# A pairwise bilinear kernel: when the first store of a group leaves, and its last three fields sent in nine row slices

## The chip, the cores and the metric

The kernel runs on one core of one Trainium2 chip. The metric is the device time of one execution in microseconds. Three runs of the kernel before gave 1286.73, 1286.80 and 1287.43 us; the median is 1286.8 us. One further execution was profiled; it took 1287.24 us.

## What is computed

The input `x` holds 4096 samples of 32 fields with 64 numbers each, in float32, and `W` is a 64 x 64 matrix. For each pair of fields i < j the output is the product, number by number, of field i with field j times W:

```
vid = jnp.einsum('bfd,de->bfe', x, W)
idx_i, idx_j = jnp.triu_indices(F_, k=1)
return x[:, idx_i, :] * vid[:, idx_j, :]
```

There are 32 * 31 / 2 = 496 pairs a sample, so the output is 15.5 times as large as the input: 520 MB are written and 33.6 MB are read.

## The kernel before

**Tiles.** The samples are cut into 16 tiles of 256. A tile lies in memory with 2 x 64 numbers of the embedding on the 128 partitions (two half-batches of 128 samples share a tile) and 128 samples along a row. One field of a tile is then a unit of 128 partitions x 512 bytes, 64 KB. The one buffer `mem` has 445 such units on the chip. It holds inputs (32 units a tile, at the places of `XPLACE`) and outputs (at the places of `SLOTS`) together, and parts of it are used again and again.

**Work of a tile.** Eight matmuls (line 172) multiply 32 fields by a matrix that has W twice on its diagonal, into `vid` in PSUM. Then VectorE (DVE in the profile) makes the 496 products (line 196), several pairs in one instruction, in an order given by `by_block`. It writes them into the output slots one after another. When a slot is full (`at == end`), one transfer from SyncE's queue (SP) takes it to the output (line 199). `SLOTS` lists 70 slots of 32 to 127 units with their places in `mem`; a third number in an entry is a seam, at which DVE's instructions are split. A slot's place is written again as soon as the stores that read it, as far as they overlap the new piece, have landed.

**Loads.** The tiles are loaded in three groups (`GROUPS`): tiles 0 to 5 at the start, tiles 6 to 10 when tile 4's products are issued, and tiles 15 to 11 later on. A group's load is cut in pieces (`CUTS`), each piece a transfer of its own (line 153). The pairs of numbers in `CUTS` are ranges of units of the group: the last load of the first group, 64 units, goes as 38 and 26; the second group's 160 units as 127, 7 and 26; the third's as 127, 7 and 26 from the top down.

**Order around the change.** The orders of SP's and DVE's instructions are as written in the program (`manual_schedule`). SP issues all transfers, loads and stores, in one queue. After a group's load, `pieces` holds its transfers, and the first store that follows gets an extra dependency by `behind(store, pieces[-2])`: it is issued only when the last piece but one has landed. At this point one piece, 26 units, is still on its way. `pieces` is then emptied, so no other store has such a wait. In what follows, the three places where a load is followed by such a store are called boundaries. The stores concerned are slot 0 (96 units), slot 22 (96 units) and slot 44 (120 units).

The framework gives every transfer a semaphore that tells of its landing. In the trace, 81 transfers (11 loads and 70 stores) use eight semaphores by turns. Each landing counts 16, one for each DMA engine.

Of the kernel before, what the change touches and what calls it, by code (L numbers as in the profile page):

```python
# [21 lines left out]
    [[6, 7, 8, 9, 10]],  # L22
    [[15, 14, 13, 12, 11]],
]
CUTS = [[None, [(0, 38), (38, 64)]], [(0, 127), (127, 134), (134, 160)], [(33, 160), (26, 33), (0, 26)]]
XPLACE = [317, 349, 381, 413, 32, 0, 285, 317, 349, 381, 413, 128, 96, 64, 32, 0]


# [9 lines left out]
    (126, 247), (127, 96), (109, 223), (112, 333), (127, 158), (127, 285), (127, 64, 94),  # L38
    (127, 192, 93), (124, 320), (120, 48), (127, 190), (124, 317), (125, 158),
]  # L40


PAD = 24
# [9 lines left out]
def by_block():  # L53


    def within(lo):
        yield "step", lo, 2, 1, 0
        for k in range(2):
            yield "step", lo, 4, 2, k
        for i in (lo, lo + 8):  # L60
            yield "row", i + 4, i, 4, 4
        yield "row", lo + 8, lo, 8, 8

    yield from within(0)
    yield "row", 16, 0, 16, 16
    yield from within(16)


def products(blocks, at=0):

    for kind, a, b, c, d in blocks:
        if kind == "row":
            rows, n, i0, di, j0, dj = c, d, b, 0, a, 1
        else:
            rows, n, i0, di, j0, dj = 16 // b, c, a, b, a + c + d, b
        r = k = 0
        while r < rows:
            room = BREAKS[bisect_right(BREAKS, at)] - at
            if k or room < n:
                m, w = 1, min(n - k, room)  # L80
            else:
                m, w = min(rows - r, room // n), n
            yield at, m, w, i0 + r * di + k, di, j0 + r * dj, dj
            at += m * w
            if k + w == n:
                r, k = r + m, 0
            else:
                k += w
# [10 lines left out]
@with_exitstack  # L99
def pairwise_bilinear_kernel(  # L100
    ctx: ExitStack,
    tc: tile.TileContext,
    x0: bass.AP,
    x: bass.AP,
    out: bass.AP,
):

    nc = tc.nc
    NT = sum(len(tiles) for group in GROUPS for tiles in group)
    F = x0.shape[1] - 1 - PAD0
    D = P // 2
    NP = F * (F - 1) // 2

    BANK = 512 // C


    ctx.enter_context(tc.manual_schedule(engines={mybir.EngineType.SP, mybir.EngineType.DVE}))

    const = ctx.enter_context(tc.tile_pool(name="const", bufs=1))
    psum = ctx.enter_context(
        tc.tile_pool(name="ps", bufs=1, space=bass.MemoryType.PSUM)
    )
    vid = psum.tile([P, F, C], F32)

    mem = const.tile([P, UNITS, C], F32)


    w2 = const.tile([P, P], F32)


    place = XPLACE[0]
    nc.sync.dma_start(
        out=mem.rearrange("p u c -> p (u c)")[:, place * C - D : (place + F // 2) * C],
        in_=x0.rearrange("p u c -> p (u c)")[:, C - D : (1 + F // 2) * C],
    )
    nc.sync.dma_start(out=mem[:, place + F // 2 : place + F, :], in_=x0[:, 1 + F // 2 : 1 + F, :])  # L140
    nc.vector.memset(w2, 0.0)  # L141
    for half in (slice(0, D), slice(D, P)):
        nc.vector.tensor_copy(w2[half, half], mem[half, place - 1, C - D :])  # L143
    loaded = 1

    def load(tiles, cuts=()):
        nonlocal loaded
        n = len(tiles) * F
        place = XPLACE[tiles[0]]
        at = (loaded - 1) * F  # L150
        loaded += len(tiles)
        return [
            nc.sync.dma_start(out=mem[:, place + lo : place + hi, :], in_=x[:, at + lo : at + hi, :])  # L153
            for lo, hi in cuts or [(0, n)]
        ]

    ready = mybir.DependencyInfo(mybir.DependencyClass.Sync, mybir.DependencyReason.DATA)

    def behind(later, earlier):
        tc.add_manual_dep(later.ins, earlier.ins.name, ready, reason="issued when that has landed")  # L160

    pieces = []
    groups, cuts = iter(GROUPS), iter(CUTS)
    for tiles, parts in zip(next(groups)[1:], next(cuts)):
        pieces = load(tiles, parts)

    for t in range(NT):
        xt = mem[:, XPLACE[t] : XPLACE[t] + F, :]


        for b in range(0, F, BANK):
            nc.tensor.matmul(  # L172
                vid[:, b : b + BANK, :],
                lhsT=w2,
                rhs=xt[:, b : b + BANK, :],
                start=True,
                stop=True,
            )

        for at, m, w, i, di, j, dj in products(by_block(), t * NP):  # L180
            slot = bisect_right(STARTS, at) - 1
            n = m * w
            begin, end = STARTS[slot], STARTS[slot + 1]
            ot = mem[:, SLOTS[slot][1] : SLOTS[slot][1] + SLOTS[slot][0], :]
            o = ot[:, at - begin : at - begin + n, :]
            if m == 1:
                left = xt[:, i : i + w, :]
                right = vid[:, j : j + 1, :].to_broadcast([P, w, C])
            else:
                o = o.rearrange("p (m w) c -> p m w c", m=m)  # L190
                right = vid[:, j : j + (m - 1) * dj + 1 : dj, :].unsqueeze(2).to_broadcast([P, m, w, C])
                if di == 0:
                    left = xt[:, i : i + w, :].unsqueeze(1).to_broadcast([P, m, w, C])
                else:
                    left = xt.rearrange("p (m d) c -> p m d c", d=di)[:, i // di : i // di + m, i % di : i % di + w, :]
            nc.vector.tensor_tensor(o, left, right, ALU.mult)  # L196
            at += n
            if at == end:
                store = nc.sync.dma_start(out=out[:, begin:end, :], in_=ot)  # L199
                if pieces:  # L200
                    behind(store, pieces[-2])
                    pieces.clear()


        if t + 2 == loaded < NT:
            (tiles,) = next(groups)
            pieces = load(tiles, next(cuts))
# [45 lines left out]
```

## Time and profile before

| | |
|---|---|
| median of three runs | 1286.8 us |
| the profiled execution, its own time | 1287.24 us |
| its span, first to last instruction | 1285.5 us |
| DVE busy | 1084.0 us (84%), 348 instructions |
| TensorE (PE) busy | 231.1 us (18%) |
| transfers' packets and bytes | 11,664 packets, 553.7 MB |
| chain that ended last | DVE 47%, DMA 44%, issue 6% |
| DVE's waits for stores | 164.2 us, 33 times, longest 21.8 us |

The times are microseconds from the start of the span. "Landing" is when a transfer's semaphore has reached its value; since 16 engines carry a transfer and each reports for itself, a transfer has 16 landings, and their spread is how far the engines have drifted apart. A packet is what one engine moves in one go, here one row of a transfer: a transfer of 128 rows gives each of the 16 engines eight packets. The trace has the start, duration and size of each packet, but not the number of its engine. A transfer's issue on SP (some 0.3 us) is not the transfer itself, which goes on long after.

The three boundaries in the trace, in us:

| | first store issued | load's last piece landed, first to last engine | first store landed, first to last engine |
|---|---|---|---|
| first | 28.78 | 31.99 to 33.91 | 46.45 to 48.42 |
| second | 426.51 | 429.45 to 432.34 | 443.98 to 446.92 |
| third | 829.50 | 831.80 to 834.84 | 849.93 to 852.96 |

### The profile page before, as it was taken

The numbers are of one execution on the slowest core, as the hardware profiler recorded it, in microseconds if no ns is written. First come the engines' busy times: TensorE is split into PE (matmuls) and PEld (weight loads), VectorE is DVE, ScalarE is ACT, GpSimd is POOL, SyncE is SP. The second block draws the span as 40 slices with busy tenths as digits, with TensorE's granted clock in tenths as the row PEclk, the third lists the DMA queues.
The fourth block names the chain that finished last, engine by engine and source line by source line (L and its number), as shares of the span: only waits on it lengthen the run. The fifth ranks groups of instructions, "written<-read, shape, count | busy, mean of one in ns | idle before, by whom it ended". The sixth has DMA issues, their size and how long they took to land.

```text
span 1285.5 us, 1143 instructions
## 1 busy us (share of the span) xinstructions
PE 231.1 (18%) x256; PEld 67.7 (5%) x256; DVE 1084.0 (84%) x348; POOL 0.2 (0%) x4
## 2 busy tenths in 40 slices
PE   5031121303120212040311211103122130312000
PEld 1000000100000000010000000000000010000000
DVE  6889998899967389899799992849998889999952
POOL 0000000000000000000000000000000000000000
PEclk8555565556555556555565555556555555555555
DMA  9999999999999999999999999999999999999998
GB/s 400 438 429 438 436 428 438 431 435 436 432 430 439 416 433 425 445 430 433 439 427 441 435 429 436 419 432 429 440 432 440 429 430 441 429 441 430 434 436 370
DMA packets 11670, 553.75 MB, mean 431 GB/s; under 512 B 1296, under 2 KB 1296, under 8 KB 1552
## 3 DMA queue, kind: packets, MB, share of 16 engines
q1 hardware_dynamic: 11664, 553.69, 99.8%
q8 instruction: 2, 0.03, 0.0%
q14 instruction: 4, 0.03, 0.0%
HBM read 33.59 MB, written 520.09 MB: 431 GB/s over the span
## 4 chain that ended last, share of the span: by engine, by line
DVE 47%; DMA 44%; issue 6%; PE 0%; DVEq 0%; SPq 0%
DVE mem L196 47%; DMA out_dram<-mem 41%; DMA mem<-in_r_x_dram 3%; PE vid L172 0%; DVEq L241 0%; DVEq L196 0%; DVE w L143 0%; SPq L153 0%; DVEq L143 0%; SPq L199 0%
## 5 line engine op out<-in xcount | busy, mean ns | idle before, releaser
L196 DVE TENSOR_TENSOR mem<-mem,vid 128x1024 f32<-128x1024 f32 (+17 forms) x345 | 1083.4, 3212 | 170.5 <-DMA out_dram<-mem 164.2
L172 PE MATMUL vid<-mem,w 128*128 128x512 f32 x256 | 231.1, 1039 | 951.3 <-DVE mem L196 843.8
L172 PEld LDWEIGHTS vid<-mem,w 128*128 128x128 f32 x256 | 67.7, 306 | 1113.5 <-DVE mem L196 1011.9
L143 DVE COPY w<-mem 64x64 f32<-64x64 f32 x2 | 0.4, 190 | 5.0 <-DMA mem<-in_r_x_dram 4.9
L141 DVE MEMSET w<- 128x128 f32 x1 | 0.2, 165 | 0.8 <-PEq L221 0.8
L221 POOL MEMSET const-bfloat16-1.0<- 128x1 bf16 x1 | 0.1, 101 | 0.0
L221 POOL MEMSET const-uint8-127<- 128x1 uint8 x1 | 0.1, 101 | 0.0
L221 POOL MEMSET const-float32-0.0<- 128x1 f32 x1 | 0.1, 98 | 0.2 <-issue 0.2
L221 POOL MEMSET const-float32-1.0<- 128x1 f32 x1 | 0.1, 98 | 0.0
## 6 DMA issues: line engine op xcount, KB each, us to landing
out_dram<-mem SPq DMA_DIRECT2D x15, 8128.0 KB, 27.4
out_dram<-mem SPq DMA_DIRECT2D x14, 7680.0 KB, 24.9
out_dram<-mem SPq DMA_DIRECT2D x6, 7168.0 KB, 26.2
out_dram<-mem SPq DMA_DIRECT2D x5, 7936.0 KB, 28.2
out_dram<-mem SPq DMA_DIRECT2D x3, 7424.0 KB, 22.6
out_dram<-mem SPq DMA_DIRECT2D x3, 5888.0 KB, 20.9
mem<-in_r_x_dram SPq DMA_DIRECT2D x2, 8128.0 KB, 37.6
out_dram<-mem SPq DMA_DIRECT2D x2, 8064.0 KB, 24.3
```

The source lines that it names most:

```text
L141: nc.vector.memset(w2, 0.0)
L143: nc.vector.tensor_copy(w2[half, half], mem[half, place - 1, C - D :])
L172: nc.tensor.matmul(vid[:, b : b + BANK, :], lhsT=w2, rhs=xt[:, b : b + BANK, :], start=True, stop=True,)
L196: nc.vector.tensor_tensor(o, left, right, ALU.mult)
L221: nc = _bacc.Bacc("TRN2", target_bir_lowering=False, num_devices=1, dynamic_dma_scratch_size=512)
```

## The change

It has two parts. The cuts of the loads move, so that the last piece, which is still on its way when the first store is issued, has 13 units at the first boundary and 20 at the others, in place of 26; the second piece of the later groups has 13 units in place of 7. And the first store of each group, the one with the extra dependency, is cut in two: all units but the last three go out in one transfer of 128 partitions, and the last three in nine transfers that take 64, 14, 12, 10, 8, 8, 6, 4 and 2 partitions (together 128). The nine follow in SP's program right behind the main transfer. The extra dependency is on the main transfer alone. All other stores stay as they are. The kernel then has 108 transfers in place of 81.

```diff
-CUTS = [[None, [(0, 38), (38, 64)]], [(0, 127), (127, 134), (134, 160)], [(33, 160), (26, 33), (0, 26)]]
+CUTS = [[None, [(0, 51), (51, 64)]], [(0, 127), (127, 140), (140, 160)], [(33, 160), (20, 33), (0, 20)]]
...
+TAIL = 3
+ROWS = [64, 14, 12, 10, 8, 8, 6, 4, 2]
...
             if at == end:
-                store = nc.sync.dma_start(out=out[:, begin:end, :], in_=ot)
+                cut = SLOTS[slot][0] - (TAIL if pieces else 0)
+                store = nc.sync.dma_start(out=out[:, begin : begin + cut, :], in_=ot[:, :cut, :])
+                if begin + cut < end:
+                    for lo, n in zip(accumulate([0, *ROWS]), ROWS):
+                        rows = slice(lo, lo + n)
+                        nc.sync.dma_start(out=out[rows, begin + cut : end, :], in_=ot[rows, cut:, :])
                 if pieces:
                     behind(store, pieces[-2])
                     pieces.clear()
```

## The prediction

> **What bounds the kernel now.** I read the queue table first, because the strip of 40 slices shows the DMA engines at 9 in all slices but the last.
>
> ```profile
> q1 hardware_dynamic: 11664, 553.69, 99.8%
> HBM read 33.59 MB, written 520.09 MB: 431 GB/s over the span
> ```
>
> One queue carries every load and store, and its packets fill 99.8% of 16 engines' span. A packet of 65,024 bytes takes 2.40 us by the packet records (27 GB/s an engine), so the bytes alone set the time. The packet times sum to 1282.4 us an engine; with each size at its usual (20th percentile) duration they would sum to 1278.3. So 4.1 us is all that can come from faster packets. Some more lies in skew: the 16 landings of one transfer spread, 0.8 us in the first loads and 2.88 us (1281.72 to 1284.60) in the last store. The slowest engine sets the end.
>
> Next the chain of waits, for the places where a load hands over to the first store of a group (three "boundaries").
>
> ```profile
> 12.52 16.27 DVE mem L196 x7
> 28.78 19.64 DMA out_dram<-mem
> 48.42 0.03 issue
> ```
>
> The store leaves at 28.78 and the last engine's part lands at 48.42. DVE's data was ready earlier: what held it was the load, as SP's own waits say.
>
> ```profile
> SPq L199 <- DVE mem L196: 1104.4, 67, 32.5
> SPq L199 <- DMA mem<-in_r_x_dram: 96.8, 3, 35.8
> ```
>
> Three waits for a load, one a boundary; all other stores wait for DVE. The issues around the boundaries:
>
> ```profile
> 28.78 0.35 SPq L199 DMA_DIRECT2D out_dram<-mem  x1
> ...
> 41.95 0.34 SPq L199 DMA_DIRECT2D out_dram<-mem  x1
> ```
> ```profile
> 426.51 0.82 SPq L199 DMA_DIRECT2D out_dram<-mem  x2
> ```
> ```profile
> 833.50 0.34 SPq L199 DMA_DIRECT2D out_dram<-mem  x1
> ```
>
> The second store of a group is issued at 41.95, 426.91 and 833.50: 6.5, 20.0 and 19.5 us before the first store's last landing (48.42, 446.92, 852.96). So today the engines pass from the first store to the second without a hole. Last, line 199 in the view by source line:
>
> ```profile
> L199 SPq DMA_DIRECT2D out_dram<-mem x70: 332/332/423, 28.8 to 1260.2; - x70
> L199 SPq EVENT_SEMAPHORE  x60: 17/17/28, 28.7 to 1229.7; - x60
> ```
>
> The reader is to see 60 small waits, each over in 17 ns. The records tell what they are: the 81 transfers raise eight semaphores in strict turn (100, 101, 103 to 108), and SP waits for the transfer eight places back on the same semaphore before it issues, unless it has waited for that one already. With big stores that transfer landed long ago.
>
> **What the Trainium skill says.** "DMA: Bandwidth & Descriptors", section "Why a DMA increments its semaphore by 16 and not by 1": a transfer from SP runs on the largest number of engines up to 16 that divides its slowest dimension, and takes the lowest-numbered ones. So 64 rows give every engine 4, and 14, 12, 10, 8, 8, 6, 4 and 2 give one row each to the lowest 14, 12 and so on: the lowest two engines get 12 rows, the highest two 4, in place of 8. The trace of before has only 128-row transfers and can't confirm it. Same page, "Anatomy of one DMA": a transfer's semaphore rises only after the last byte's receipt. The trace agrees: landings come 0.37 us (median; 0.27 to 1.05) after the packet's end. Same page, "Latency and other measured facts": about 0.6 us from issue to first byte. The trace says more: the first load is issued at 0.73, its first packets start from 1.74 to 2.37, 1.0 to 1.64 us later. I use the trace.
>
> **The change, part by part.**
>
> *The cuts.* With 26 fields left, the last piece (8 packets of 13,312 bytes an engine, 495 ns at best) lasts 3.96 us. Its packets take 551 ns in the mean, because from about 1.2 us after the store's issue they run up to 1.05 us long. The slowest engine's landings show the loss. First boundary: 33.91 - (28.69 + 3.96) = 1.26 us. Second: 432.34 - (426.45 + 3.96) = 1.93. Third: 834.84 - (829.44 + 3.96) = 1.44. After the issue the load has 3.96 - 0.37 (landing) - 1.2 = 2.4 us to run beside the store. With 13 left (1.98 us) that is 0.4 us, with 20 left (3.05 us) 1.5 us. In proportion the losses become 0.2, 1.2 and 0.9, so the slowest engine **gains** 1.05, 0.75 and 0.55: 2.35 us in all. Fast engines wait some tenths for the later store; they lead, so this hides. Bounds: 0 to 4.63 us (the whole loss). The middle piece grows from 7 to 13 fields, still one transfer.
>
> *The nine transfers, as work.* The main store loses 3 fields: 8 packets by 57 ns an engine, 0.45 us. They come back as packets of 1536 bytes, which I put at 65 ns from the 3584-byte row (140 ns): 0.26 us on the highest engines, 0.78 on the lowest. The sum of work stays within 0.1 us. SP's issues of the first seven, at 0.33 to 1.27 us (the longest issue in this trace, a load's), take 2.4 to 9 us under a main store of 14.1 us (93 fields) or 17.7 us (third boundary): nothing on the path.
>
> *The nine transfers, as places in the turn.* This is what costs. Main store is place n, the transfers n+1 to n+9. Transfers 1 to 6 meet landed transfers, or at most the load piece that all wait for. Transfer 7 meets the last load piece, a matter of tenths. **Transfer 8 (4 partitions) meets the main store itself**, transfer 9 the first transfer. So SP stands at transfer 8 until the main store has landed on its slowest engine, and the group's second store, ready long before, stands behind it in the same program. The engines have nothing but transfers 1 to 7 left, and run dry. On the first boundary's clock: the main store lands at 48.42 - 0.45 = 47.97 (less the gain of the cuts). Two issues with their waits, 0.39 each, and one more wait: the second store is issued at 48.8. First packets 1.0 to 1.64 us later; I take 1.3: 50.1. Refill of the engines after the hole: at the kernel's start the packets of the first 20 us run 0.73 us an engine over the usual; with large packets I take 0.3, between 0 and 0.73. In before, the slowest engine begins the second store at 48.07 (48.42 less 0.35). So 2.3 us a boundary, three times 6.9. Bounds: 1.6 a boundary (shortest issue and arrival, no refill) to 3.2 (longest): 4.9 to 9.5.
>
> *What moves with it.* DVE's next work waits for the first store's buffer, whose main part is free up to 1.5 us earlier; the operation that writes the last three fields runs 12 us later (60.8 against 48.5 at the first boundary), past the landing of transfers 8 and 9 near 49 to 50. The third store is issued at 61.5, over 5 us before the delayed second store ends (50 + 18). Nothing new is late. The hole also lines the engines up, which takes the lead from the fast ones but not time from the slowest. The shifted turn of eight meets only old stores later.
>
> *Sum.* 6.9 - 2.35 = 4.5 us. The profiled execution took 1287.24 (span 1285.5, the rest around it), 0.4 over the median of 1286.8; the same difference on the median gives 1291.3, +0.35%.
>
> **Rivals.**
> *A, no dry engines, so faster.* The turn would have to spare transfer 8, for instance with more semaphores. For it: the waits of before never cost time. Against it: eight numbers for 81 transfers, without exception. Then the cuts' 2.35 us and four fewer rows on the slowest engines (4 by 57 ns, three times: 0.7) are a gain: 1283.8. It decides if the second store is issued before the first has landed.
> *B, the hole is paid for by the cuts.* The slow packets vanish wholly (4.63) and the hole is at its lowest (4.9): 1287.1, no change. It needs holes of 1.6 us and load packets all near their best.
> *C, a restart as at the kernel's start.* Longest arrival and 0.73 us of refill, no gain from the cuts, which the hole's lining-up may swallow: +9.5, 1296.3.
>
> **How the numbers follow.** Forecast 0.63, A 0.09, B 0.14, C 0.14. A measurement of this kernel can tell about 0.2% (2.6 us) from no change: 1284.2 to 1289.4. Faster: most of A, 0.06. Same: the rest of A, B, and a tail of the forecast, 0.20. Slower: 0.74. Range from B's 1287.0 to just over C, 1296.5; A and half of B's spread stay outside.
>
> **What would show it.** The view by line: SP waiting at the store lines for a store of its own, three waits of some 6 to 15 us, and three stretches of 2 us with the DMA share near zero about 47, 446 and 852. The second store's issue after the first's landing. The 16 landings of later stores spread by 1 us, not 3. Load packets of the last piece near their best. If the second store leaves early, I am wrong and A holds; if holes are there but the time is unchanged, the cuts gave more than I took.

## The result, and the profile after

The changed kernel takes 1295.99 us (median of five; 1295.92 to 1296.37) against 1287.43 us for the kernel before on the same chip: +8.6 us, ratio 1.0072 with a 95% interval of 1.0061 to 1.0084. The forecast was slower by 4.5 us; it is slower by nearly twice that.

The queue table of the changed kernel's page. Columns are packets, MB and the packets' share of 16 engines' span.

```profile
q1 hardware_dynamic: 12288, 553.69, 99.3%
q8 instruction: 2, 0.03, 0.0%
q14 instruction: 5, 0.03, 0.0%
HBM read 33.59 MB, written 520.09 MB: 428 GB/s over the span
```

The bytes are the same and the share falls from 99.8% to 99.3%. Of a span of 1294.3 us an engine is without a packet for 9.3 us in the mean, where it was 3.0 before; the packets' own time is 1285.1 us an engine, 2.6 more than before. The lines q8 and q14 are fetches of instructions. They look like nothing, but they matter below.

SP's waits in the changed kernel (us in total, times, longest). Line 204 issues the whole stores and the main part of the split ones, line 208 the nine small transfers.

```profile
SPq L204 <- DVE mem L200: 1050.3, 64, 30.4
SPq L204 <- DMA mem<-in_r_x_dram: 102.7, 3, 37.8
SPq L208 <- DMA out_dram<-mem: 30.4, 3, 12.4
```

The last line is the wait of transfer 8 for the main store, once a boundary. SP's timeline at the first one (start, duration, line, number of issues):

```profile
30.74 0.35 SPq L204 DMA_DIRECT2D out_dram<-mem  x1
31.13 16.21 SPq L208 DMA_DIRECT2D out_dram<-mem  x9
47.44 0.36 SPq L204 DMA_DIRECT2D out_dram<-mem  x1
```

The group's second store leaves at 47.44, after the first has landed (46.77), where the kernel before sent it at 41.95. The stretches of 1 us about that time, first of the changed kernel, then of the one before; the last two columns are the DMA share (packets count where they start, so it can pass 1) and GB/s.

```profile
46.00:47.00 1.00, 0.00 (x0) 0.00 (x0) 0.13 (x1) 0.00 (x0) 0.50 0.55 159
47.00:48.00 1.00, 0.00 (x0) 0.00 (x0) 1.00 (x1) 0.00 (x0) 0.50 0.03 9
48.00:49.00 1.00, 0.00 (x0) 0.00 (x0) 1.00 (x2) 0.00 (x0) 0.50 2.30 983
```
```profile
46.00:47.00 1.00, 0.00 (x0) 0.00 (x0) 0.00 (x0) 0.00 (x0) 0.50 1.62 700
47.00:48.00 1.00, 0.00 (x0) 0.00 (x0) 0.00 (x0) 0.00 (x0) 0.50 0.85 369
```

So the hole is there, as forecast, at all three boundaries. But it isn't the whole loss. I took for each 128-row transfer the last of its 16 landings, the slowest engine's, and subtracted that of the kernel before (a fetch is dated by the clock of the kernel that it hits):

| where, us in the kernel before | changed kernel, lateness of the slowest engine | what happens there |
|---|---|---|
| 48 to 67, first boundary | +0.48 at its end | hole, less the cut's gain |
| 127 to 146 | 0.71 to 1.66 | fetch of instructions at 134.7 |
| 388 to 406 | 1.65 to 2.49 | from stores to loads |
| 425 to 465, second boundary | 2.49 to 3.97 | hole, less the cut's gain |
| 539 to 558 | 4.27 to 5.17 | fetch at 550.4 |
| 791 to 828 | 5.14 to 6.39 | from stores to loads |
| 828 to 870, third boundary | 6.39 to 6.73 | hole, less the cut's gain |
| 898 to 909 | 6.81 to 7.78 | fetch at 909.7 |
| 927 to 945 | 7.77 to 7.11 | the kernel before is hit itself (fetch at 930.7) |
| 1025 to 1043 | 7.13 to 9.00 | fetch of 16 KB at 1049.8 |
| end | 8.68 | |

The boundaries with their holes and their gains make 2.3 us. The steps far from them make 6.4: fetches 4.03 (0.95 + 0.90 + 0.97 - 0.66 + 1.87), changes from stores to loads 2.09, the rest drift (the lateness creeps up by 0.23, 0.31 and 0.08 after the three holes and falls by 0.32 near the end; why is not shown). The spread of the 16 landings shows why the steps reach the slowest engine. After the first hole it is 0.18 us, where the kernel before has 1.99; after the second 0.30 against 2.92; after the third 0.20 against 3.02. A fetch is one packet. The queue table of the changed kernel for 134 to 136 us:

```profile
q1 hardware_dynamic: 16, 1.04, 121.3%
q14 instruction: 1, 0.01, 1.0%
```

It takes 0.31 us on one engine, and two data packets of that time are 0.27 and 0.36 us over their usual 2.40: together 0.94. In this transfer's landings the last engine falls 0.95 back, and the spread goes from 0.20 to 1.09. In the kernel before, a fetch is there too, at 151 us, with a packet stretched by 0.29 and one by 0.35, and the last landing doesn't move. The queue table of the kernel before for 150 to 152 us:

```profile
q1 hardware_dynamic: 14, 0.89, 103.6%
q14 instruction: 1, 0.01, 1.0%
```

The trace has no engine numbers, but the packets of one engine join end to start, so the engine that is hit can be followed. In the kernel before its stretched packet begins at 148.62 and the slowest engine's packet of the same round at 150.43: the engine leads by 1.8 us and loses 0.95 of it. In the changed kernel the stretched packet begins at 131.99, and all 16 engines begin theirs between 131.91 and 132.09: there is no lead to lose. In the same way the fetch of 16 KB at 983.9 in the kernel before falls on an engine that lands 3.1 us ahead of the last, and leaves it 1.4 us ahead. The page "DMA: Bandwidth & Descriptors" of the Trainium skill, section "Queues, rings and completion order", says that row 14 of the queues is the runtime's own, for refill among other things; this agrees with the label of q14 here (the fetches of 16 KB are on q8 and have the same label).

**Theory L**: the spread of 2 to 3 us is room. Whatever delays an engine that leads costs nothing as long as it doesn't become the last. The hole lines all engines up, and then each fetch and each change from stores to loads counts. **Rival W**: the 6.4 us come from the 27 small transfers themselves, their issues, semaphores and the shifted turn. **Rival H**: each hole costs about 3 us by itself, wherever it stands. The table can't decide between them; the experiments do. The kernel before took 1286.8 to 1286.9 us in them, and 1287.43 beside the changed kernel, so a difference between an experiment and the changed kernel is uncertain by some 0.5 us. Readings of landings come from one profiled execution of each kernel, up to 0.7 us from its median.

### The profile page after: what moved, and what is told of

Its sections match the earlier page's. It is cut to its first block, busy times and chain, and to the rows that moved or that the text cites. A ratio compares the mean times of both kernels' runs of the same rounds, so it can differ in the third digit from the quotient of the medians.

```text
span 1294.3 us, 1190 instructions
## 1 busy us (share of the span) xinstructions
PE 231.0 (18%) x256; PEld 67.1 (5%) x256; DVE 1084.1 (84%) x348; POOL 0.2 (0%) x4
## 3 DMA queue, kind: packets, MB, share of 16 engines
q1 hardware_dynamic: 12288, 553.69, 99.3%
## 4 chain that ended last, share of the span: by engine, by line
DMA 50%; DVE 42%; issue 5%; SPq 0%; DVEq 0%
DVE mem L200 42%; DMA out_dram<-mem 41%; DMA mem<-in_r_x_dram 8%; DVEq L250 0%; SPq L157 0%; SPq L208 0%; DVEq L200 0%; SPq L144 0%; SPq L140 0%; SPq L204 0%
```

## Experiments

**Six transfers in place of nine.** From the changed kernel:

```diff
-ROWS = [64, 14, 12, 10, 8, 8, 6, 4, 2]
+ROWS = [80, 14, 12, 10, 8, 4]
```

> The changed kernel, but its last three fields go out in six transfers of 80, 14, 12, 10, 8 and 4 partitions, so that the group's second store is the seventh transfer after the first and no semaphore of the turn belongs to the store just ahead. Theory L (the holes line the engines up, and what then hits one engine or all of them at once reaches the slowest): no hole, engines keep some drift, 1285 to 1288 us. Rival W (the small transfers themselves cost: their issues of 1.2 us, their semaphores, the shifted turn): 18 of 27 of them are left, so two thirds of the 6.4 us that the holes don't explain, 1291 to 1293 us.

Measured: 1288.41 us, ratio 1.0012 (1.0005 to 1.0018). That is 7.6 us under the changed kernel. From the first store's landing to the second's the slowest engine's lateness grows by 0.73, 0.36 and 0.66 at the three boundaries, where it was 2.13, 2.67 and 2.15 with nine transfers; the 0.45 of the three fields that moved are in all of these. So the holes are gone, and most of the loss with them. The second store is issued at 42.09, before the first has landed (46.69):

```profile
42.09 0.36 SPq L204 DMA_DIRECT2D out_dram<-mem  x1
```
```profile
SPq L204 <- DMA out_dram<-mem: 27.7, 3, 12.9
```

SP still waits for a first store three times, but only ahead of the third store, the eighth transfer behind it, and then the second store is already in the queue. The time is 0.4 us over L's range, and below W's.

**The cuts alone.** From the kernel before, the new `CUTS` line only.

> The new cuts alone, no small transfers. The forecast's step for the cuts says 2.35 us less, 1285.0 us. From the landings of the last pieces in the changed kernel the gain on the slowest engine is 3 to 4 us, 1283 to 1284 us. Theory L: part of that is given back, because engines that end together have less lag to hide a later hit, 1284.5 to 1287.5 us. W says 1283 to 1285 us.

Measured: 1287.01 us, ratio 1.0001 (0.9993 to 1.0010). The gain is there and goes again: the slowest engine is 1.24 us ahead at 127 us. Its engines are then only 0.32 apart, and over the transfer with a fetch, seen in the queue table of 150 to 154 us,

```profile
q1 hardware_dynamic: 31, 1.97, 114.2%
q14 instruction: 1, 0.01, 0.5%
```

the lead falls from 1.23 to 0.35. At the change to loads near 405 us it turns into 0.38 of lateness. At the end 0.22 of the lead are left. This is what L says, not the forecast's 2.35.

**The nine transfers alone**, with the old cuts.

> The nine transfers alone, with the old cuts. Holes as in the changed kernel, after load pieces that are slowed as in the kernel before. L: the slowest engine loses the cuts' 3.4 us again, 1297 to 1300 us. W: the same or 1297 us. It mainly says how much of the cuts' gain comes through when there are holes.

Measured: 1298.6 us, ratio 1.0091 (1.0077 to 1.0105), 2.6 over the changed kernel and inside L's range; W allowed this time too. With holes the cuts are worth something; without them, nothing.

**The wait alone.** From the kernel before: no cuts, no small transfers; the second store of each group waits for the landing of the first.

```diff
+    first = []
...
+                if first:
+                    behind(store, first.pop())
                 if pieces:
                     behind(store, pieces[-2])
                     pieces.clear()
+                    first.append(store)
```

> Old cuts, whole stores, no small transfer; only the wait is added: the second store of each group is issued when the first has landed. The holes are some 0.6 us shorter than with transfers 8 and 9 in the way. L: three holes of about 1.3 us, and the hits that reach lined-up engines, about 6 us less what the old cuts' drift hides again: 1292 to 1297 us. W: three holes alone, 1290.5 to 1292 us.

Measured: 1297.28 us, ratio 1.0080 (1.0067 to 1.0092): +10.3 us, with the transfers of the kernel before, 0.3 us over L's range. SP's waits in this kernel, and its stretch from 46 to 48 us with no packet starting:

```profile
SPq L200 <- DMA mem<-in_r_x_dram: 98.4, 3, 36.6
SPq L200 <- DMA out_dram<-mem: 61.1, 3, 22.3
```
```profile
46.00:48.00 2.00, 0.00 (x0) 0.00 (x0) 0.00 (x0) 0.00 (x0) 0.50 0.00 0
```

Three waits, and the whole loss is there without one added transfer: W falls. The holes are 1.52, 1.56 and 1.54 us on the slowest engine's landings; its lateness is 9.35 at the end. Between the holes the same steps appear as in the table: 0.92 at each of two fetches, 1.6 at that of 16 KB, 0.9 and 0.7 at the changes to loads. It is even dearer than the changed kernel, which has the cuts' gain.

**A hole at the first boundary only.** From the wait alone:

```diff
-                    first.append(store)
+                    if t < 5:
+                        first.append(store)
```

> Before, with one hole only: at the first boundary the second store waits for the first one's landing. Theory L: the hole costs 1.5 us on the slowest engine, and until the second boundary, where the old cuts pull the engines apart again, the next instruction fetch adds 0.9 and the change from stores to loads 0.9: 2.5 to 3.5 us over before. Rival H (each hole costs the same by itself, a third of the 10 us of the kernel with three): 3.3 us.

Measured: 1290.12 us, ratio 1.0026 (1.0015 to 1.0037), +3.2. L and H meet here, so the time doesn't tell them apart. The landings do: 1.52 at the hole, 0.92 at the fetch of 154.6 us, 1.73 at one of 16 KB at 331.6. The 0.9 that I expected at the change from stores to loads doesn't come (4.06 before it and after it): the fetch of 16 KB has left the engines 2.0 us apart. Then the old cut pulls the engines 2.75 us apart, and for the next 350 us, two fetches among them, the lateness stays between 3.5 and 3.7.

**A hole near the end only.** From the kernel before:

```diff
+                if slot == len(SLOTS) - 2:
+                    behind(store, last)
+                last = store
```

> Before, with one hole only, near the end: the last store but one waits for the landing of the store ahead of it. After it no fetch and no load comes. L: the hole alone, 1.2 to 1.8 us over before. H: a third of the three holes, 3.3 us.

Measured: 1288.32 us, ratio 1.0012 (1.0006 to 1.0019), +1.4. SP's waits there:

```profile
SPq L199 <- DMA mem<-in_r_x_dram: 97.3, 3, 36.4
SPq L199 <- DMA out_dram<-mem: 34.1, 1, 34.1
```

The same hole, 1.51 us on the landings (0.87 ahead before it, 0.64 late after it), with nothing behind it to hit lined-up engines. H said 3.3.

**Two holes a group.** The third store waits for the second as well. From the kernel before:

```diff
+    first = []
...
+                if first:
+                    behind(store, last)
+                    first.pop()
+                last = store
                 if pieces:
                     behind(store, pieces[-2])
                     pieces.clear()
+                    first.extend((1, 2))
```

> Two holes a group: the second store waits for the first and the third for the second, old cuts. L: the engines are lined up after the first hole already, so the second one costs its own length alone, 1.5 us three times: 4 to 5.5 us over the kernel with one hole a group, 1301 to 1303 us. H: each further hole costs as much as the first ones did, 3.3 us: 1307 us.

Measured: 1301.22 us, ratio 1.0112 (1.0098 to 1.0126), 3.9 over the kernel with one hole a group (4.6 between the two traces). The second holes are 1.49, 1.54 and 1.52 us on the landings: each costs its own length, once the engines stand in line. H said 10.

**One hole a group, with the new cuts**, no small transfers.

> One hole a group as in the kernel with holes alone, but with the new cuts; no small transfers. L: with the engines lined up by the hole anyway the cuts' gain on the slowest engine comes through, 2.5 to 3.5 us under the kernel with holes alone: 1293.5 to 1295 us. If the cuts are worth nothing, as they were without holes: 1297 us. Against the changed kernel this leaves out the 27 small transfers: up to 2 us less, since transfers 8 and 9 lengthen each hole by some 0.6 us.

Measured: 1294.71 us, ratio 1.0060 (1.0047 to 1.0074), 2.6 under the wait alone. This is the changed kernel without its 27 small transfers: it is 7.8 us over the kernel before, the changed kernel 8.6. So the transfers themselves cost 0.8 us (1.3 by the two times as they are), and the wait that they bring the rest.

**The new cut at one boundary only**, at the third, at the first, and at the third with 13 fields. From the kernel before, one entry of `CUTS` each; for the last:

```diff
-[(33, 160), (26, 33), (0, 26)]
+[(33, 160), (13, 33), (0, 13)]
```

> Before, with the new cut at the third boundary alone (20 fields left). Theory L: the lag that the first two boundaries leave stays and hides the fetches and the change to loads up to there; after the third boundary only two or three fetches come. Of the 1.2 us that the cut gains there most is kept: 0.5 to 1.2 us under before, 1285.7 to 1286.4 us. Rival (a cut's gain is always given back): no change, 1286.9 us.

> Before, with the new cut at the first boundary alone (13 fields left). L: 1.2 us gained at the boundary, 0.9 lost at the next instruction fetch near 150 us and the rest at the change from stores to loads near 405 us; the old cut at the second boundary then pulls the engines apart as before: 0.3 us under to 0.6 over, 1286.6 to 1287.5 us. If the gain of a cut were kept: 1285.7 us.

> Before, with the last piece of the third load cut to 13 fields. L: the load's slow packets vanish nearly (1.4 us gained on the slowest engine), the engines are then closer together and the later fetches reach the slowest one: 0.3 to 1.2 us under before. If 13 is too late, the engines stand dry for some tenths before the store and it is 1287 us.

Measured: 1286.57 (0.9998; 0.9989 to 1.0006), 1287.51 (1.0006; 0.9998 to 1.0014) and 1287.59 us (1.0007; 1.0001 to 1.0014). None is faster. The first of them was meant to keep its gain, and I expected 0.5 to 1.2 us less. In its profiled execution (1287.14 us, over its median) the slowest engine is 1.05 us ahead at 1025 us, with the engines 1.13 apart, and then this packet comes (queue table from 1040 to 1046 us of that kernel):

```profile
q1 hardware_dynamic: 62, 2.97, 114.8%
q8 instruction: 1, 0.02, 1.0%
```

It turns the lead into 0.24 of lateness. In the kernel before that fetch came at 983.9, with the engines 3.6 apart, and left no mark. So here the rival's line was the right one, by L's mechanism. With the cut at the first boundary alone the slowest engine is 1.38 us ahead at 127 us, 0.53 after the fetch at 151.5 and 0.25 late after the change to loads near 405. With 13 fields at the third boundary I expected 0.3 to 1.2 us less, and it is 0.8 more: there the slowest engine is 0.97 ahead at 1025, with the engines 0.76 apart, and the fetch of 16 KB at 1041.4 makes it 0.63 late. No version beats the kernel before by more than a measurement can tell.

## Why the prediction was wrong

**Right: the wait and its place.** Transfer 8 waits for the main store, the second store behind it leaves after the landing, and the engines run dry. All three holes are where they were put (near 47, 449 and 858 us in the changed kernel, for 47, 446 and 852 on the clock of the kernel before).

**Right in kind: the size at the boundaries.** The holes were put at 2.3 us each, 6.9. Measured on the slowest engine, from the first store's landing to the second's and less the 0.45 of the three fields that moved, they are 1.68, 2.22 and 1.70: 5.6. The terms that were too long, at the first boundary: first packets come 0.85 to 1.00 us after the start of the issue (47.44 to 48.29 and 48.44), not 1.3; transfers 8 and 9 take 0.30 and 0.35 with their waits (46.79 to 47.44), not 0.39 each; the refill is hardly to be seen (first packets of 2.29 to 2.31 us for the usual 2.27). At the second boundary 0.46 us pass between SP's last wait and the issue of the second store (448.82 to 449.28), 0.05 at the others; the records don't say why. The Trainium skill's figure for issue to first byte, about 0.6 us ("DMA: Bandwidth & Descriptors", "Latency and other measured facts"), is still below the trace. The section "Anatomy of one DMA" of that page, which the prediction names for the receipt, describes transfers issued from GpSimd; that it fits SP's transfers here rests on the trace's landings. The cuts' gain was put at 1.05, 0.75 and 0.55; the last pieces' landings give 1.24, 0.72 and 1.41, 3.4 in place of 2.35. So the boundaries net 2.3, not 4.5.

**Wrong: the step "What moves with it".** This is the step that failed. It said that the hole "lines the engines up, which takes the lead from the fast ones but not time from the slowest". The same lead was used in the cuts' step ("they lead, so this hides"), but not asked for afterwards, and its loss was put at nothing. The lead hides more than a late store: fetches that hold one engine up by 0.9 or 1.9 us, and the load packets' arrival among stores. Without it 6.4 us more are lost, three fourths of the result. The runs with holes alone show it without any other part of the change; the hole near the end shows that a hole by itself costs 1.5 us, and that the rest comes from what follows it; the cuts alone show it the other way round, as a gain that is eaten.

**Wrong: the value of the cuts.** The 2.35 were a gain on the path in the sum, and 4.1 us was named as all that faster packets could bring. Where no hole lines up the engines anyway, they bring nothing (1.0001). What the slow load packets cost the slowest engine is lead for the others: after the first boundary the engines are 1.99 us apart in the kernel before, 0.59 with the cuts alone.

**The rivals.** A (no dry engines, faster) is what the six transfers come nearest to; the engines don't run dry, yet it is 0.12% slower, not faster. B (no change) is out. C's number, 1296.3, is within 0.4 of the measured 1295.99, but not by its reasons: arrival and refill are short, and the cuts' gain comes through.

**Rows.** Whether moving rows from high to low engines evens anything out stays open: with six transfers the slowest engine is 1.1 us later at the end than with the cuts alone, and the trace has no engine numbers. **Fetches.** That a fetch is the cause of its step is read from times and joined packets in these traces; a kernel without fetches was not tried.

## What to carry to other kernels

Ask of every added transfer which earlier transfer's semaphore it takes over: with eight in turn, the eighth transfer behind a store waits for that store, and so does all that is queued after it. In a kernel that is bound by 16 parallel engines the time is the slowest one's, and the lead of the others is the room in which everything irregular is hidden; a change that evens them out, or makes all wait for one landing, loses that room, and pays for it hundreds of microseconds later. So follow the last landing of each transfer over the whole span, not only at the place that was changed.

## What the runs showed of the hardware that was not expected

A small transfer that doesn't use all engines takes SP long to issue while a store is on its way. The view by line of the changed kernel (duration min/median/max in ns):

```profile
L208 SPq DMA_DIRECT2D out_dram<-mem x27: 252/1082/1524, 31.1 to 857.8; - x27
```

Transfers of 14, 12, 10, 8, 8 and 6 rows take 1.03 to 1.52 us each, the one of 64 rows 0.47 to 0.54, and those of 4 and 2 rows, issued when the queue has run empty, 0.25. The kernel with six transfers shows that the queue makes this difference and not the number of rows: its transfer of 4 rows is issued while the main store is on its way, and takes 1.03 to 1.11 us. First that one, then the transfer of 4 rows of the changed kernel, both at the first boundary:

```profile
36.25 1.11 SPq L208 DMA_DIRECT2D out_dram<-mem  x1
```
```profile
46.79 0.25 SPq L208 DMA_DIRECT2D out_dram<-mem  x1
```

The long issues were hidden under the main store here. The 14-row transfer's semaphore is raised once at 33.25, just after its issue ends, and 14 times between 46.79 and 47.15; this agrees with the section "Why a DMA increments its semaphore by 16 and not by 1" of the Trainium skill's page "DMA: Bandwidth & Descriptors" (only the engines used report, SP adds the rest at once).

When the first packets of a load meet the last ones of a store, lined-up engines all lose at once. Near 405 us, 16 store packets of 61,952 bytes run 0.50 to 1.08 us over their usual time in the changed kernel. In the kernel before eleven do, by 0.39 to 1.01, and the slowest engine's landing shows nothing of it.
